# One tap of a depthwise convolution moved from VectorE to ScalarE and GpSimd, inside a state-space loop

## The chip, the cores and the metric

The kernel runs on one core of a Trainium2 chip. A core has a matrix engine (TensorE, PE in the profile, with PEld for its weight loads), VectorE (DVE), ScalarE (ACT), GpSimd (POOL) and SyncE (SP, which here issues DMAs). Each engine takes its instructions in order from its own queue; between engines they are ordered by semaphores. SBUF is the working memory on the chip, PSUM the accumulator memory of TensorE, in banks of 128 partitions x 512 floats.

The metric is the device time of one execution in microseconds. A separate profiled execution gives the trace.

## What is computed

Two layers of a sequence model over x, 64 sequences of 64 positions with 256 features, all float32. The first layer is a conditioned scan and an attention over the batch, then a modulated feed-forward net with quantised weights. The second layer is a tanh recurrence followed by a selective state-space block ("mamba"), and then two mixtures of experts. The change lies in the state-space block:

```python
xz = x @ W_in
xi, z = jnp.split(xz, 2, axis=-1)
xi_t = jnp.moveaxis(xi, 1, 2)
xi_pad = jnp.pad(xi_t, ((0, 0), (0, 0), (d_conv - 1, 0)))
conv = jax.lax.conv_general_dilated(xi_pad, W_conv, ..., feature_group_count=d_inner)
xc = jax.nn.silu(jnp.moveaxis(conv + b_conv[None, :, None], 2, 1))
dbc = xc @ W_xproj
delta_lr, B, C = jnp.split(dbc, [r, r + n], axis=-1)
delta = jax.nn.softplus(delta_lr @ W_dt + b_dt)
...
dA = jnp.exp(delta[..., None] * A)
dBx = delta[..., None] * B[:, :, None, :] * xc[..., None]
...
    h = dA_t * h + dBx_t
    y = jnp.einsum('bdn,bn->bd', h, C_t) + D * x_t
...
return y * jax.nn.silu(z) @ W_out
```

The inner width is 512, there are 16 states for each inner feature, and the convolution has four taps per feature (`d_conv` is 4), over the position: the value at position t is a weighted sum of positions t, t-1, t-2 and t-3, and positions before the first are zero.

## The kernel before

The 4096 tokens are cut into 8 chunks of 512 (8 whole sequences of 64). The 512 inner features are 4 blocks of 128 partitions (`NI = 4`), handled as two pairs (`PI = 2`). Function `mamba` runs over 8 chunks x 2 pairs x 16 states = 256 state steps.

A state step, for both blocks of the pair, consists of:
- an input: GpSimd multiplies `dx` by a state's B, spread over the partitions by a DMA (`inputs`, L1048, tile `hb`, five buffers, issued two steps ahead);
- a decay: ScalarE takes the exponential of delta times A into one of three PSUM banks (`decay`, L1055, tiles `dA0` to `dA2`, issued one step ahead; two banks are used by a step, so the second decay of the next step has to wait for a scan of this one);
- two scans on VectorE (L1100), one for each block, with the decay from PSUM and `hb` from SBUF;
- a multiply of both blocks by the state's C on VectorE (L1102); C is spread by a small matmul into the bank `cb` (L1000);
- a sum over the states on TensorE: eight transposing matmuls that accumulate in the banks `yp0` and `yp1` (L1115).

Beside the steps of a chunk, the loop places pieces of other work, a few at each step (`turn`, `pieces`, `urgent`, `others`): the head of the next chunk (`head`), the gates of this one (`gates`), its end (`finish`, `project`), and the shared expert of the mixture that follows (`mix.beside`, lines L1835 to L1855). A `yield` in these helpers marks where a piece ends.

The head of a chunk makes the convolution. For each of its four blocks, two matmuls fill the bank `mp` (L919; in the loop there is one such bank). ScalarE writes the last tap and the bias to `xc` (L923, `acc`). VectorE adds the three earlier taps, each shifted by one more position, straight from the bank (L926, 504, 496 and 488 elements per partition). After the fourth block, ScalarE takes the Silu of all four blocks (L930), which needs another table of ScalarE than the exponential of the decays, so that a table load stands before it and another before the next decay (L1055). Then TensorE projects `xc` (L934), and delta is made from the projection (L951 to L974), with the temporaries `t2` and `t3`, whose pool `p1` has a single buffer for each name. At the end of each pair of blocks, ScalarE also copies the sums out of their banks (L1127, `yT`).

The head of chunk 0 runs before the loop, with nothing beside it; the heads of chunks 1 to 7 run beside the steps of chunks 0 to 6. What follows an engine in its queue is settled when the program is built: a scheduler orders the instructions from the program and its own costs. The scans and the state multiplies are kept in the order of the program by a token (`stamp_issue_order_token`).

Of the kernel before, what the change touches and what calls it, by code (L numbers as in the profile page):

```python
# [13 lines left out]
F32 = mybir.dt.float32  # L14
BF16 = mybir.dt.bfloat16
I32 = mybir.dt.int32
AF = mybir.ActivationFunctionType
# [4 lines left out]
P = 128  # L22
B, L, D = 64, 64, 256
NT = B * L
CH = 512
# [835 lines left out]
def mamba(g, w, hs, beside):  # L861
# [3 lines left out]
    nc, tc = g.nc, g.tc  # L865
# [5 lines left out]
    PI = 2  # L871
# [5 lines left out]
    seq = lambda t: t.rearrange("p (b l) -> p b l", l=L)  # L877
    with (
# [30 lines left out]
        def head(c, v):  # L909

            tok = ts(c, CH)
            v.xc = p2.tile([P, NI, CH], F32, name="xc")
            v.delta, v.dx, v.sz, v.ready = [], [], [], 0
            v.dbc = p1.tile([W, CH], F32, name="dbc")
            v.parts = parts[c % 2]
            for i in range(NI):
                ps = one()
                for k in range(KD):
                    nc.tensor.matmul(ps, w.Win[:, k, ts(i, P)], hs2[:, k, tok], start=(k == 0), stop=(k == KD - 1))  # L919
                    if k == 0:  # L920
                        yield MID
                acc = v.xc[:, i, :]
                nc.scalar.activation(acc, ps, AF.Identity, bias=w.col[:, 0, i : i + 1], scale=w.taps[:, i, 3:4])  # L923
                for s in range(1, 4):
                    to = seq(acc)[:, :, s:]
                    nc.vector.scalar_tensor_tensor(  # L926
                        to, seq(ps)[:, :, : L - s], w.taps[:, i, 3 - s : 4 - s], to, ALU.mult, ALU.add
                    )
                yield
            nc.scalar.activation(v.xc, v.xc, AF.Silu)  # L930
            yield
            ps = one()
            for i in range(NI):
                nc.tensor.matmul(ps[:W, :], w.Wxp[:, i, :], v.xc[:, i, :], start=(i == 0), stop=(i == NI - 1))  # L934
                if i < NI - 1:
                    yield MID
            nc.scalar.copy(v.dbc, ps[:W, :])

            v.B = tc.dram_tile((S, CH), F32, name=f"B{c}")
            nc.sync.dma_start(v.B, v.dbc[R : R + S, :])  # L940


            r = slice(C0, W)
            nc.scalar.copy(v.parts[32 : 32 + S, :], ps[r, :])
            nc.vector.tensor_sub(ps[r, :], ps[r, :], v.parts[32 : 32 + S, :])
            nc.scalar.copy(v.parts[0:S, :], ps[r, :])
            nc.vector.tensor_sub(v.parts[64 : 64 + S, :], ps[r, :], v.parts[0:S, :])
            yield


            for i0 in range(0, NI, PI):  # L951
                z, u = (p3.tile([P, PI, CH], F32, name=n) for n in ("delta", "dx"))
                v.delta.append(z)
                v.dx.append(u)
                t2, t3 = (p1.tile([P, PI, CH], F32, name=n) for n in ("t2", "t3"))
                for i in range(PI):
                    ps = one()
                    nc.tensor.matmul(ps, w.Wdt[:, ts(i0 + i, P)], v.dbc[:R, :], start=True, stop=True)
                    nc.scalar.activation(z[:, i, :], ps, AF.Relu, bias=w.col[:, 1, i0 + i : i0 + i + 1])
                    nc.scalar.activation(u[:, i, :], ps, AF.Abs, bias=w.col[:, 1, i0 + i : i0 + i + 1])  # L960
                    yield
                e = nc.gpsimd if c else nc.vector
                nc.scalar.activation(u, u, AF.Exp, scale=-1.0)
                nc.scalar.activation(t2, u, AF.Identity, bias=unit[:, 0:1])
                nc.scalar.activation(t3, t2, AF.Identity, bias=unit[:, 1:2])
                yield
                e.tensor_sub(u, t3, u)
                yield
                nc.scalar.activation(t2, t2, AF.Ln)
                yield  # L970
                e.tensor_add(z, z, t2)
                yield
                e.tensor_sub(z, z, u)
                e.tensor_mul(u, z, v.xc[:, i0 : i0 + PI, :])  # L974
                v.ready += PI
                yield
# [85 lines left out]
        for _ in head(0, vs[0]):  # L1062
            pass
# [22 lines left out]
        for s in range(LAST):  # L1086
            c, j = divmod(s, STEPS)
            p, n = divmod(j, S)
            now = vs[c]
            if j == 0:  # L1090
                ahead = head(c + 1, vs[c + 1]) if c + 1 < NCH else iter(())
                pieces = chain(pieces, gates(c, now, 0), islice(ahead, 3 * NI + PI + 6), gates(c, now, PI), ahead)
                left = 0
# [1110 lines left out]
```

## Time and profile before

| | us |
|---|---|
| median of 3 runs | 2761.14 (2759.80 to 2762.74) |
| the profiled execution | 2768.27 |
| its span | 2766.5 |
| VectorE busy | 1766.7 (64%) |
| ScalarE busy | 1387.4 (50%) |
| GpSimd busy | 1338.1 (48%) |
| TensorE busy | 2320.8 (84%) |
| the state loop, first scan to the end of the last steps | 698.5 to about 1815 |

The granted clock of TensorE was 0.931 of full speed in the mean over the span. The shares above are averages over very different stages: before the state loop stand the scan, the attention and the feed-forward net, after it the two mixtures of experts. In the loop VectorE is the busiest; after it, TensorE.

A row of a group is "line engine operation, output<-inputs, shapes, xcount | busy us, mean ns of one | idle time of the engine just before them, and what ended it". A row of the waits is "engine line waited for <- what ended the wait: us in total, times, longest us". A row of the stretches gives for each engine its busy time and the number of its instructions, then the granted clock of TensorE, the share of the DMA engines and GB/s.

### The profile page before, as it was taken

The numbers are of one execution on the slowest core, as the hardware profiler recorded it, in microseconds if no ns is written. First come the engines' busy times: TensorE is split into PE (matmuls) and PEld (weight loads), VectorE is DVE, ScalarE is ACT, GpSimd is POOL, SyncE is SP. The second block draws the span as 40 slices with busy tenths as digits, with TensorE's granted clock in tenths as the row PEclk, the third lists the DMA queues.
The fourth block names the chain that finished last, engine by engine and source line by source line (L and its number), as shares of the span: only waits on it lengthen the run. The fifth ranks groups of instructions, "written<-read, shape, count | busy, mean of one in ns | idle before, by whom it ended". The sixth has DMA issues, their size and how long they took to land.

```text
span 2766.5 us, 34415 instructions
## 1 busy us (share of the span) xinstructions
PE 2320.8 (84%) x11977; PEld 1662.4 (60%) x11996; DVE 1766.7 (64%) x2980; ACT 1387.4 (50%) x2300; POOL 1338.1 (48%) x1166
## 2 busy tenths in 40 slices
PE   3989967997678888887888888788876989999995
PEld 3634435774345656564555555567655778888884
DVE  0567638982999898989889897952353443333333
ACT  0567527884575858585758576543222212222220
POOL 0023345530686878786888787835455331111110
PEclk9879988997769999999999999999998999999997
DMA  9999920002112222221122222226776755555555
GB/s 225 369 360 348 297 71 1 1 1 92 61 62 76 73 73 73 73 73 65 66 96 73 88 73 95 90 92 200 240 262 216 269 216 200 197 198 202 219 194 192
DMA packets 180503, 406.06 MB, mean 147 GB/s; under 512 B 24785, under 2 KB 84434, under 8 KB 174946
## 3 DMA queue, kind: packets, MB, share of 16 engines
q1 hardware_dynamic: 166882, 366.80, 38.9%
q0 software_dynamic: 13440, 36.98, 3.5%
q8 instruction: 97, 1.59, 0.2%
q14 instruction: 84, 0.69, 0.1%
HBM read 280.76 MB, written 144.98 MB: 154 GB/s over the span
## 4 chain that ended last, share of the span: by engine, by line
PE 45%; DVE 23%; ACT 12%; issue 9%; POOL 3%; another core or an unknown queue 2%; DMA 1%; SPq 0%; DVEq 0%; ACTq 0%; POOLq 0%
DVE hb L1100 13%; PE ps L1690 11%; PE acc L1588 9%; PE out L450 4%; DVE hb L1102 4%; PE ps L1657 2%; PE yp L1115 2%; ACT dA L1055 2%; PE mq L1835 2%; DVE xc L926 1%; PE s L416 1%; PE acc L441 1%; ACT L1055 1%; PE ps L1698 1%
## 5 line engine op out<-in xcount | busy, mean ns | idle before, releaser
L1048 POOL TENSOR_TENSOR hb<-dx,Bn 128x1024 f32<-128x1024 f32 x256 | 604.7, 2377 | 233.5 <-PE yp L1115 189.3
L1100 DVE TENSOR_TENSOR_SCAN hb<-dA,hb 128x512 f32<-128x512 f32 x512 | 602.1, 1208 | 62.0 <-ACT dA L1055 60.7
L1055 ACT ACTIVATE dA<-delta,negA 128x504 f32<-128x504 f32 x512 | 343.9, 682 | 284.9 <-DVE hb L1100 275.7
L1115 PEld LDWEIGHTS yp<-ident,hb 128*128 128x128 f32 x2048 | 261.1, 149 | 169.4 <-issue 134.9
L1102 DVE TENSOR_TENSOR hb<-hb,cb 128x1024 f32<-128x1024 f32 x256 | 311.9, 1219 | 44.1 <-PE cb L1000 25.1
L1690 PE MATMUL ps<-gxT,w 128*128 128x256 f32 (+1 forms) x1600 | 324.5, 361 | 1.4 <-DVE gxT L1565 0.8
L1690 PEld LDWEIGHTS ps<-gxT,w 128*128 128x128 f32 x1600 | 276.3, 190 | 47.6 <-issue 12.7
L1115 PE MATMUL yp<-ident,hb 128*128 128x128 f32 x2048 | 296.0, 288 | 0.0
L1835 PE MATMUL mq<-x,moe_s 128*128 128x256 f32 x896 | 242.3, 404 | 54.1 <-ACT up L1842 29.5
L1364 POOL DMA_INDIRECT ffn_y<-gy,to x72 | 69.3, 962 | 432.6 <-ACT gy L1590 420.1
L1835 PEld LDWEIGHTS mq<-x,moe_s 128*128 128x128 f32 x896 | 166.8, 199 | 120.8 <-ACT up L1842 35.8
L1694 DVE TENSOR_TENSOR gh<-gs,ps 128x256 f32<-128x256 f32 (+1 forms) x200 | 78.5, 394 | 212.5 <-ACT gs L1693 203.7
L1590 ACT ACTIVATE gy<-acc,wt 128x256 f32<-128x256 f32 x152 | 67.2, 473 | 250.4 <-PE acc L1588 224.2
L1588 PE MATMUL acc<-w,gh 128*128 128x256 f32 (+1 forms) x864 | 191.0, 392 | 0.0
L1693 ACT ACTIVATE gs<-ps 128x256 f32<-128x256 f32 (+1 forms) x200 | 72.2, 363 | 233.7 <-PE ps L1690 220.7
L1000 PE MATMUL cb<-parts,pick 80*128 80x512 bf16 x256 | 104.2, 407 | 87.0 <-DVE hb L1102 82.1
L1588 PEld LDWEIGHTS acc<-w,gh 128*128 128x128 f32 (+1 forms) x864 | 147.2, 192 | 31.0 <-issue 13.4
L432 POOL TENSOR_TENSOR E<-E,z 128x1024 f32<-128x1024 f32 x32 | 61.6, 1926 | 194.2 <-DVE z L431 111.4
L1364 POOL DMA_INDIRECT moe_y<-gy,to x80 | 77.6, 970 | 103.4 <-ACT gy L1590 79.4
L1588 PE MATMUL acc<-w,rh 128*128 128x256 f32 x320 | 86.0, 410 | 44.3 <-ACT rh L1659 41.5
L450 PE MATMUL out<-oT,hs 128*128 128x512 f32 x256 | 117.8, 604 | 1.5 <-ACT oT L443 1.5
L1578 DVE TENSOR_REDUCE wt<-pick 128x2 f32<-128x4 f32 (+1 forms) x88 | 13.6, 155 | 162.5 <-ACT gy L1590 144.0
(475 smaller groups left out, 4436.6 us busy)
## 6 DMA issues: line engine op xcount, KB each, us to landing
w<-ffn_w SPq DMA_DIRECT2D x40, 2176.0 KB
Bn<-B SPq DMA_DIRECT2D x128, 512.0 KB
moe_x<-fill SPq DMA_DIRECT2D x130, 260.0 KB
ffn_x<-fill SPq DMA_DIRECT2D x129, 260.0 KB
w<-moe_w SPq DMA_DIRECT2D x48, 512.0 KB
ffn_w<-in_ffn_W_dram SPq DMA_DIRECT2D x16, 640.0 KB
gx<-moe_x SPq DMA_DIRECT2D x32, 260.0 KB
gx<-ffn_x SPq DMA_DIRECT2D x32, 260.0 KB
```

What stands on the lines that cost most here:

```text
L450: nc.tensor.matmul(ps, M[:, o, ts(k, P)], v.o[:, o], start=(o == 0), stop=(o == H // 2 - 1))
L1000: nc.tensor.matmul(t, pick[:, n : n + 1].to_broadcast([rows, P]), v.parts, start=True, stop=True)
L1048: nc.gpsimd.tensor_mul(hb, vs[c].dx[p], Bn[:, n % NB, :].unsqueeze(1).to_broadcast([P, PI, CH]))
L1055: nc.scalar.activation(decays[s][i][:, :, 1:], seq(vs[c].delta[p][:, i, :])[:, :, 1:], AF.Exp, scale=A[:, p * PI + i, n : n + 1],)
L1100: ins = nc.vector.tensor_tensor_scan(h, dA[i].rearrange("p b l -> p (b l)"), h, 0.0, ALU.mult, ALU.add)
L1102: ins = nc.vector.tensor_tensor(hb, hb, cb.unsqueeze(1).to_broadcast([P, PI, CH]), ALU.mult)
L1115: nc.tensor.matmul(yp[i][:, t, :], hb[:, i, ts(t, P)], g.ident, start=(n == 0 and t == 0), stop=(n == S - 1 and t == CH // P - 1), is_tran ...
L1364: i = self.g.nc.gpsimd.indirect_dma_start(out=self.y, out_offset=bass.IndirectOffsetOnAxis(ap=to, axis=0), in_=y, in_offset=None)
L1588: nc.tensor.matmul(po[s], h, w, start=(i == 0), stop=(i == n - 1))
L1690: nc.tensor.matmul(ps[:, j, :], v.w12[:, k, ts(j * (full + 1) + i, P)], v.xT[:, k, :], start=(k == 0), stop=(k == KD - 1))
L1694: nc.vector.tensor_mul(v.h[:, i, : v.rows], s, ps[:, 1, :])
L1835: nc.tensor.matmul(ps[:, i % 2, :], w[:, k, ts(i, P)], xu[:, k, :], start=(k == 0), stop=(k == KD - 1))
```

## The change

In the heads of chunks 1 to 7 the first of the three taps (shift by one position, 504 elements) is no longer added by VectorE. ScalarE multiplies the bank by the tap's weights into a temporary `q`, which takes the buffers of `t2` (blocks 0 and 2) and `t3` (blocks 1 and 3). VectorE adds the other two taps as before. After the `yield`, so in a later piece, GpSimd adds the temporary to `xc`. The head of chunk 0 (`c` is 0) stays as it was.

```diff
                 acc = v.xc[:, i, :]
                 nc.scalar.activation(acc, ps, AF.Identity, bias=w.col[:, 0, i : i + 1], scale=w.taps[:, i, 3:4])
-                for s in range(1, 4):
+                many = 1 if c else 0
+                q = p1.tile([P, PI, CH], F32, name=("t2", "t3")[i % 2]) if c else None
+                for s in range(1, 1 + many):
+                    to = seq(q[:, s - 1, :])[:, :, s:]
+                    nc.scalar.activation(to, seq(ps)[:, :, : L - s], AF.Identity, scale=w.taps[:, i, 3 - s : 4 - s])
+                for s in range(1 + many, 4):
                     to = seq(acc)[:, :, s:]
                     nc.vector.scalar_tensor_tensor(
                         to, seq(ps)[:, :, : L - s], w.taps[:, i, 3 - s : 4 - s], to, ALU.mult, ALU.add
                     )
                 yield
+                for s in range(1, 1 + many):
+                    to = seq(acc)[:, :, s:]
+                    nc.gpsimd.tensor_add(to, to, seq(q[:, s - 1, :])[:, :, s:])
             nc.scalar.activation(v.xc, v.xc, AF.Silu)
```

Since the addition of the fourth block stands after its `yield`, it is written in the same piece as the Silu behind it, which reads what the addition wrote. The scheduler orders the whole program anew, so instructions near the head can stand in another order on every engine; line numbers behind the change grow by 8 (the scan is L1108, the Silu L938).

## The prediction

> **What bounds the kernel now.** I read the stretches of the state loop first, then the waits inside it, then the chain of waits through one head. The loop runs from 698.5 to 1815 us of a span of 2766.5.
>
> ```profile
> core 0: us, PE busy (x) PEld busy (x) DVE busy (x) ACT busy (x) POOL busy (x), PEclk, DMA share, GB/s
> 977.00:1116.00 139.00, 119.00 (x570) 79.57 (x569) 125.57 (x119) 99.53 (x134) 108.47 (x53) 0.99 0.21 73
> ...
> 1009.00:1047.00 38.00, 31.74 (x154) 21.43 (x153) 36.87 (x38) 26.88 (x35) 23.66 (x12) 1.00 0.16 56
> ```
>
> The first row is a whole chunk, the second the part of it in which the convolution of the next chunk's head runs. VectorE is busy 90% of the chunk and 97% of the convolution. TensorE follows with 84%, GpSimd has 62% there and ScalarE 71%.
>
> ```profile
> ACT dA L1055 <- DVE hb L1100: 275.7, 261, 5.4
> POOL hb L1048 <- PE yp L1115: 189.3, 97, 6.2
> DVE hb L1100 <- ACT dA L1055: 60.7, 41, 5.4
> DVE hb L1102 <- PE cb L1000: 25.1, 24, 3.2
> ```
>
> These are the waits inside the loop: total us, times, longest. ScalarE and GpSimd mostly wait for VectorE and for what follows it (275.7 and 189.3 us). VectorE itself waits 60.7 us for a decay, in 41 places. So VectorE sets the pace, except where ScalarE is held by something long.
>
> ```profile
> 1009.09 1.22 DVE hb L1102
> 1010.31 0.65 DVE xc L926
> 1010.96 1.13 DVE hb L1100
> 1012.09 0.63 DVE xc L926
> ...
> 1039.65 0.57 ACT dA L1055
> 1040.27 0.58 ACT yT L1127
> 1040.87 1.28 ACT L930
> 1042.16 1.91 ACT xc L930
> 1044.07 0.47 ACT yT L1127
> 1044.56 1.28 ACT L1055
> 1045.86 0.69 ACT dA L1055
> ...
> 1046.64 2.35 DVE hb L1100 x2
> ```
>
> This is the chain through that head (start, us, what). The taps (L926) stand on it, between scans and multiplies. Then it passes to ScalarE: table load, Silu of xc, table load back, decay. VectorE reaches the scan at 1046.64 only 0.44 us before that decay is there, so the last taps hide nearly all of the Silu block. That cover is what the change takes from.
>
> **The change, part by part.** Durations are of the profiled execution.
>
> ```profile
> L926 DVE SCALAR_TENSOR_TENSOR xc<-mp,taps,xc 128x504 f32<-128x504 f32 x28 | 20.3, 724 | 0.0
> L923 ACT ACTIVATE xc<-mp,mcol,taps 128x512 f32<-128x512 f32 x28 | 21.5, 769 | 11.5 <-PE mp L919 11.5
> L959 ACT ACTIVATE delta<-mp,mcol 128x512 f32<-128x512 f32 x28 | 19.0, 680 | 6.9 <-PE mp L958 6.9
> L1011 POOL TENSOR_TENSOR xc<-xc,sz 128x512 f32<-128x512 f32 x30 | 38.2, 1275 | 1.6 <-DVE xc L1010 1.6
> ```
>
> *Removed.* The 504-wide tap goes in the heads of chunks 1 to 7, four times each: 28 instructions (the head of chunk 0, ahead of the loop, keeps its three). Records overlap a little, so I count what the chain gives one tap before the next instruction, 0.62 to 0.75 us, mostly 0.65: 28 x 0.65 = 18.2 us. By the row's mean it would be 20.3 us, the most that can be had.
>
> *Added on ScalarE.* 28 scaled copies out of the bank. None is in the trace: below it stands the plain copy L1127 (0.58), above it L923 with a scale and a bias (0.77). I take 0.70, by L959 and by the decay L1055 (504 wide, scale, 0.68): 28 x 0.70 = 19.6 us. Over the convolution ScalarE waits 10.1 us for VectorE in front of decays, and that hides most of it; without this cover all 19.6 us would count. It is not hidden where ScalarE is just coming out of a table reload: in heads 2 to 4 after the shared expert's Silu (L1846, at 1014.59), where the built order puts a copy (and another bank read) ahead of the second decay; in heads 5 and 6 in the gate's Silu block, where the copy stands between the two loads. One copy each: 5 x 0.70 = 3.5 us lost. Bounds: 0 and 7 x 0.77 = 5.4.
>
> *Added on GpSimd.* 28 additions over 8 rows of 63. By L1011 and L1843, 512 wide, 1.27 us; bounded below by 0.95 (half of L432's 1.93 for 1024) and above by 2.37 (L1048, 1024 wide). I take 1.27, the nearest width: 35.6 us on a queue that idles 191.4 us in the loop before its multiplies. Scans wait for GpSimd 0.8 us in all, so the multiplies run well ahead and delay nobody. Behind an addition in the queue stand state multiplies (two steps ahead of need), the shared expert's L1843, and the convolution's own later additions. The third and fourth scaled copies wait until the first and second additions have let go of the temporary; in the built order some two state steps (over 7 us) lie between, against 3.6 us for a multiply and an addition: nothing.
>
> *The new wait.* The Silu of xc no longer waits for the last tap but for the last GpSimd addition, and ScalarE stands in order: behind Silu are two copies, the table reload and the next decay, for which the scan waits. No DMA moves, and no queue of SyncE is passed. I follow the built order from the scan (time 0) that frees the bank of the last decay before the block. VectorE then has a multiply, two scans, a multiply and a scan before it needs the first decay behind the block: 5 x 1.13 = 5.65 us, and each tap in between adds 0.64. ScalarE needs 0.05 + 0.69 + 1.28 + 1.91 + 2 x 0.58 + 1.28 + 0.69 = 7.06 us.
> In heads 2 to 4 both last taps now lie before time 0. GpSimd then has multiply, L1843, multiply and addition in a row (its buffers come free 2 us after each state multiply), so the addition ends at about 2.5 where Silu could start at 2.0: 0.5 us of wait. VectorE idles 7.06 + 0.5 - 5.65 = 1.9 us against 0.44 now: 1.4 lost, three times, 4.2.
> Head 1 has no copies of yT in the block and both last taps inside it (cover 6.9); the last tap ends at 2.4, the addition at 3.7, Silu at 5.6, the decay at 7.6: 0.7 lost against no idle now.
> Head 5: cover 6.3, chain 7.06 + 2 x 0.58 = 8.2, idle 1.9 against 2.31 at 1327.88: 0.4 won.
> Head 6: the shared expert's Silu and this one now stand in one block (one pair of table loads fewer): 7.06 + 1.91 + 0.58 = 9.55 against a cover of 6.9, idle 2.65, now 0.30: 2.3 lost.
> Head 7: the same block plus 1.0 us of wait for the addition, idle 3.65, now 3.53: 0.1 lost.
> Together 4.2 + 0.7 - 0.4 + 2.3 + 0.1 = 6.9 us.
>
> *Sum.* 18.2 - 3.5 - 6.9 = 7.8 us less. The profiled execution took 2768.27 us (span 2766.5), so it would take 2760.5; the median of the runs shown is 7.1 us below the profiled one, 2761.1, and becomes 2753.3.
>
> *A rule against it.* VectorE's scans took 1184 to 1225 ns and the state multiplies 1197 to 1223 throughout, while GpSimd was busy 108 of 139 us: no VectorE instruction was held up. The Trainium skill, Perfetto Trace Analysis, section Optimizing Scalar/DVE Operations, warns that moving work between GpSimd and VectorE might not help, because they share a read port of the SBUF. Its page SBUF — State Buffer, section SBUF: two separate sides, restricts the lock to VectorE instructions with two SBUF inputs or in a 2-port mode; the scan, the state multiply and the taps each read one operand from PSUM, and by that rule, too, the sum above stands. By the general warning it would come out as the last rival.
>
> **The rivals.** *The whole tap is won.* If the static order lets VectorE start its next work earlier and the Silu block finds other cover, all 18.2 us come: 2743. For it: 97% busy in the convolution. Against it: 0.44 us of slack in the block.
> *All given back.* If every head pays the worst of heads 2 to 6, that is 2.3 us in the Silu block, and a copy of 0.70 shows at one or two places, a head loses 2.3 to 3.7 of its 2.6: net about 0, 2761. TensorE, 84% busy over the convolution, can take part in this: where the taps gave it time, the state multiply would wait for its broadcast (L1000; 25.1 us now).
> *Slower: Silu stands behind GpSimd's queue.* The multiply ahead of the last addition waits for TensorE to empty its buffer. Such waits happen 97 times, 2.0 us in the mean and 6.2 at most, and I counted only a free buffer after 2 us. If the addition comes 2.4 us later in each head (one more L1048 ahead of it, or one such wait), ScalarE stands, the decay is late, and with 7 x 2.4 = 16.8 us the kernel is 9 us slower: 2770. It decides from 1.1 us a head on (7.8 / 7). For it: GpSimd is busy without a gap before the last addition in my count, and an addition of 2.37 us alone, two of them in that run, would bring 2.2. Against it: GpSimd sits idle 6.6 us in this part today.
> *The port is shared after all.* If each addition held a VectorE instruction for its 1.27 us, 35.6 us would be added: 2789. The even durations above speak against it.
> *Not doing what it says* has no chance of its own: the built program has 28 taps fewer on VectorE and 28 copies and additions more.
>
> **How the numbers follow.** Small gain (2750 to 2755.6) 0.47; whole tap 0.10; given back 0.24; slower by Silu's wait 0.16; port 0.03. A measurement of this kernel can tell about 0.2%, 5.5 us, from no change. So faster 0.57, same 0.24, slower 0.19. The range 2744 to 2770 leaves out the port, half of the slower case and a little of the whole tap; the cost bounds above (tap 20.3, copies 0 or 5.4, addition 0.95 or 2.37) stay inside it.
>
> **What would show it.** L926's successor with 68 instead of 96 instructions and VectorE about 18 us less busy in the loop; ScalarE's wait for VectorE falling by some 15 us; VectorE's wait for decays rising from 60.7 to about 70; scaled copies near 0.70 and additions near 1.27 us; Silu waiting under 1 us for GpSimd. Wrong would be additions above 2 us, waits of Silu above 1.1 us a head, or longer scans while GpSimd runs.

## The result

The changed kernel takes 2753.39 us in the median (2736.54 to 2763.35) against 2759.68 us before (2751.03 to 2763.21), 21 runs each. The medians differ by 6.3 us; 7.8 us less had been forecast. The ratio is 0.9973 with a 95% interval of 0.9960 to 0.9985, which is 4 to 11 us less. Here and below the ratio is an estimate of its own with an interval, and not quite the quotient of the two medians (0.9977 here). The forecast time of 2753.3 us is met to 0.1 us by chance: its base, 2761.1 us, was 1.4 us too high and its gain 1.5 us too large. The profiled execution of the changed kernel took 2753.39 us (span 2751.5), 15 us less than the one before. Only 6.8 us of this lie in the state loop, as the sums over its eight chunks show, cut from the loop's first scan to its last. The first is before, the second after:

```profile
sum 1114.60, PE 909.22 PEld 613.98 DVE 1005.70 ACT 749.70 POOL 867.03; mean PE 113.65 PEld 76.75 DVE 125.71 ACT 93.71 POOL 108.38
```

```profile
sum 1107.80, PE 902.00 PEld 612.62 DVE 988.91 ACT 759.82 POOL 900.54; mean PE 112.75 PEld 76.58 DVE 123.61 ACT 94.98 POOL 112.57
```

VectorE is busy 16.8 us less (1005.70 - 988.91). The loop is only 6.8 us shorter, so VectorE idles 10.0 us longer: this is the price. The other 8 us of the difference between the two profiles lie outside the loop, where the program is the same.

The groups of instructions in the loop after the change:

```profile
L937 POOL TENSOR_TENSOR xc<-xc,t 128x504 f32<-128x504 f32 x28 | 35.1, 1254 | 14.3 <-DVE xc L931 14.3
L931 DVE SCALAR_TENSOR_TENSOR xc<-mp,taps,xc 128x496 f32<-128x496 f32 x28 | 20.1, 719 | 0.0
...
L928 ACT ACTIVATE t<-mp,taps 128x504 f32<-128x504 f32 x28 | 18.8, 672 | 0.8 <-POOL xc L937 0.8
L938 ACT ACTIVATE xc<-xc 128x2048 f32<-128x2048 f32 x7 | 13.4, 1914 | 5.4 <-POOL xc L937 5.4
```

A scaled copy (L928) takes 0.672 us, an addition (L937) 1.254. The Silu (L938) now waits for the addition: 5.4 us in all, in five of seven heads. The waits of the loop:

```profile
ACT dA L1063 <- DVE hb L1108: 258.6, 241, 5.4
POOL hb L1056 <- PE yp L1123: 130.8, 65, 4.7
DVE hb L1108 <- ACT dA L1063: 67.7, 43, 5.4
DVE hb L1110 <- PE cb L1008: 24.7, 23, 3.2
```

ScalarE and GpSimd wait less than before (258.6 for 275.7, 130.8 for 189.3), since they have the added work. VectorE's wait for decays rises from 60.7 to 67.7 us. With its wait for ScalarE's `parts` in front of the split of the projection (L953; 2.8 us in place of 0.7) that is 9.1 of the 10.0 us. The place of it is seen in the chain through the head that the prediction followed (start, us, what):

```profile
1033.56 0.65 DVE xc L931
1034.21 1.13 DVE hb L1108
1035.34 0.62 DVE xc L931
1035.96 1.14 DVE hb L1108
...
1037.19 1.23 DVE hb L1110
1038.42 0.03 POOLq L1056
1038.45 0.83 POOL xc L937
1039.30 1.92 ACT xc L938
1041.22 0.95 ACT yT L1135 x2
1042.19 0.98 ACT L1063
...
1043.49 0.69 ACT dA L1063
1044.21 1.24 DVE hb L1108
```

Before, the chain went from the taps to ScalarE; now GpSimd's addition stands between them. VectorE idles 1.09 us ahead of the scan at 1044.21, against 0.44 before (the number in brackets is the idle time before an instruction):

```profile
1044.21 1.23 DVE L1108 TENSOR_TENSOR_SCAN hb<-dA,hb 128x512 f32<-128x512 f32 x1 [1.09 <-ACT dA L1063]
```

The chunk table below shows which other heads lose time.

### The profile page after: what moved, and what is told of

It is laid out like the page before. It is cut to its first block, busy times and chain, and to the rows that moved or that the text cites. A ratio compares the mean times of both kernels' runs of the same rounds, so it can differ in the third digit from the quotient of the medians.

```text
span 2751.5 us, 34452 instructions
## 1 busy us (share of the span) xinstructions
PE 2310.7 (84%) x11996; PEld 1659.9 (60%) x11996; DVE 1752.4 (64%) x2952; ACT 1398.3 (51%) x2324; POOL 1371.9 (50%) x1194
## 4 chain that ended last, share of the span: by engine, by line
PE 46%; DVE 22%; ACT 11%; issue 9%; POOL 4%; DMA 2%; another core or an unknown queue 1%; SPq 0%; DVEq 0%; ACTq 0%; POOLq 0%
DVE hb L1108 13%; PE ps L1698 11%; PE acc L1596 9%; PE out L450 4%; DVE hb L1110 3%; PE ps L1665 2%; PE mq L1843 2%; PE yp L1123 2%; ACT dA L1063 2%; PE steps L820 1%; PE s L416 1%; POOL hb L1056 1%; PE acc L441 1%; PE ps L1706 1%; PE mp L919 1%
## 5 line engine op out<-in xcount | busy, mean ns | idle before, releaser
L1056 POOL TENSOR_TENSOR hb<-dx,Bn 128x1024 f32<-128x1024 f32 x256 | 604.9, 2376 | 178.2 <-PE yp L1123 130.8
L1108 DVE TENSOR_TENSOR_SCAN hb<-dA,hb 128x512 f32<-128x512 f32 x512 | 602.3, 1210 | 68.5 <-ACT dA L1063 67.7
L1063 ACT ACTIVATE dA<-delta,negA 128x504 f32<-128x504 f32 x512 | 345.0, 685 | 265.4 <-DVE hb L1108 258.6
L1123 PEld LDWEIGHTS yp<-ident,hb 128*128 128x128 f32 x2048 | 260.1, 149 | 158.4 <-issue 125.2
L1110 DVE TENSOR_TENSOR hb<-hb,cb 128x1024 f32<-128x1024 f32 x256 | 312.4, 1220 | 45.1 <-PE cb L1008 24.7
L1123 PE MATMUL yp<-ident,hb 128*128 128x128 f32 x2048 | 294.6, 286 | 0.0
L1843 PE MATMUL mq<-x,moe_s 128*128 128x256 f32 x896 | 238.2, 399 | 57.8 <-ACT sh L1847 25.8
L1843 PEld LDWEIGHTS mq<-x,moe_s 128*128 128x128 f32 x896 | 164.3, 196 | 124.1 <-ACT sh L1847 42.9
L1008 PE MATMUL cb<-parts,pick 80*128 80x512 bf16 x256 | 103.3, 404 | 89.2 <-DVE hb L1110 83.3
L1859 PE MATMUL mq<-moe_s,sh 128*128 128x256 f32 x448 | 113.3, 386 | 6.6 <-ACT up L1850 2.9
```

Source lines behind the costliest of these rows:

```text
L1008: nc.tensor.matmul(t, pick[:, n : n + 1].to_broadcast([rows, P]), v.parts, start=True, stop=True)
L1056: nc.gpsimd.tensor_mul(hb, vs[c].dx[p], Bn[:, n % NB, :].unsqueeze(1).to_broadcast([P, PI, CH]))
L1063: nc.scalar.activation(decays[s][i][:, :, 1:], seq(vs[c].delta[p][:, i, :])[:, :, 1:], AF.Exp, scale=A[:, p * PI + i, n : n + 1],)
L1108: ins = nc.vector.tensor_tensor_scan(h, dA[i].rearrange("p b l -> p (b l)"), h, 0.0, ALU.mult, ALU.add)
L1110: ins = nc.vector.tensor_tensor(hb, hb, cb.unsqueeze(1).to_broadcast([P, PI, CH]), ALU.mult)
L1123: nc.tensor.matmul(yp[i][:, t, :], hb[:, i, ts(t, P)], g.ident, start=(n == 0 and t == 0), stop=(n == S - 1 and t == CH // P - 1), is_tran ...
```

## The experiments

What follows an engine in its queue is settled anew for each program, so a kernel with one piece less may also stand in another order. The length of each chunk (from its first scan to the next chunk's first scan; chunk k holds the head of chunk k+1, the last chunk holds none) tells where a difference arises. Two kernels with the same order up to some point agree there to about 0.1 us, as long as TensorE is not late (below). The experiments ran in three groups on three chips, on which the kernel before took 2722.05, 2759.63 and 2720.59 us. So a time is compared only with that of the kernel before in its own group; the loop of the kernel before was 1114.6 us long on the third chip too. The table is in us, from one traced execution of each kernel; all rows but the first are differences from the first:

| chunk | 0 | 1 | 2 | 3 | 4 | 5 | 6 | 7 | loop |
|---|---|---|---|---|---|---|---|---|---|
| before | 132.5 | 138.6 | 138.3 | 139.0 | 149.6 | 140.4 | 146.1 | 130.1 | 1114.6 |
| the change | -1.6 | 0.3 | -0.8 | -2.3 | -2.2 | 0.4 | 0.1 | -0.7 | -6.8 |
| heads 1 to 5 only | -2.0 | -2.4 | -1.7 | -2.4 | -3.3 | 0.0 | 0.6 | 0.1 | -11.1 |
| heads 6 and 7 only | -0.1 | 0.0 | 0.1 | -0.1 | -0.1 | 0.6 | 0.0 | -0.7 | -0.4 |
| tap gone | -2.3 | 1.5 | 2.2 | 0.9 | -1.2 | -1.0 | -3.8 | -0.7 | -4.6 |
| price alone | 2.0 | -1.0 | -0.2 | -0.5 | -1.8 | 2.2 | 4.4 | 10.0 | 15.0 |
| no wait | -1.7 | 1.9 | 1.0 | 1.3 | -3.0 | 0.6 | -2.5 | -0.6 | -2.9 |
| added twice | -2.1 | 5.1 | 5.1 | 4.4 | 2.4 | 5.5 | 5.1 | 9.7 | 35.3 |
| last block kept | -1.2 | -1.6 | -2.4 | -1.7 | -2.5 | -0.2 | -2.0 | 9.7 | -1.9 |
| no copy | -1.2 | -1.6 | -2.3 | -0.3 | -0.4 | -1.0 | 2.1 | 9.5 | 4.8 |
| last kept, table by ScalarE | -1.1 | -1.6 | -2.4 | -1.7 | -2.4 | -0.2 | -3.2 | -0.8 | -13.6 |
| the change, table by ScalarE | -1.5 | -1.0 | -1.7 | -2.4 | -2.4 | -0.4 | -0.1 | -0.8 | -10.3 |
| before, table by ScalarE | 0.0 | 0.0 | 0.1 | -0.1 | 0.0 | 0.0 | 0.7 | -0.8 | 0.0 |
| mixed, table by ScalarE | -1.9 | -2.4 | -1.7 | -2.4 | -3.3 | -0.1 | -3.1 | -0.8 | -15.7 |

### Which heads win

```diff
-                many = 1 if c else 0
+                many = 1 if 0 < c < 6 else 0
```

> The tap is moved in the heads of chunks 1 to 5 only; heads 6 and 7 keep three taps on VectorE. My theory: each head wins about 2.4 us of VectorE work (16.8 us over seven heads in the profile) and pays by its own ScalarE block; heads 6 and 7 pay about 3.0 and 2.5 us and so win nothing. Then these five heads carry the whole gain: ratio to before about 0.9975 (0.996 to 0.999), and the chunks with heads 6 and 7 are as long as before within 0.5 us. Rival (the gain is the same for every tap moved): 20 of 28 taps, 4.5 us, ratio 0.9984.

Measured: 2705.47 us against 2722.05, ratio 0.9953 (0.9936 to 0.9970). That is more gain than the range expected (0.996 to 0.999). The other part, with `many = 1 if c > 5 else 0`:

> The other part alone: the tap is moved in the heads of chunks 6 and 7 only. My theory: 4.8 us of VectorE work are won and some 5.5 us are given back because the Silu of xc now follows the shared expert's Silu in one block on ScalarE, so that the decay is later: ratio 1.0000 to 1.0005, and VectorE's idle time in those two chunks rises by 4 to 6 us. Rival (each tap gives the same): 8 of 28 taps, 1.8 us less, ratio 0.9993.

Measured: 2720.78 us, ratio 1.0000 (0.9991 to 1.0010). In the loop heads 1 to 5 bring all of the gain (11.8 us in chunks 0 to 4) and heads 6 and 7 nothing, as the theory said; in chunks 5 and 6 of the second kernel VectorE idles 5.6 us longer than before.

It was not expected that heads 1 to 5 alone win more than the whole change does there (11.8 against 6.6 us in chunks 0 to 4), though in these chunks the order of instructions is the same on every engine. The stretches show it, chunks 1 to 3 of the change first, then those of the kernel with heads 1 to 5:

```profile
831.00:969.90 138.90, 119.16 (x558) 81.11 (x558) 122.58 (x114) 100.32 (x136) 109.65 (x56) 0.95 0.21 71
969.90:1107.40 137.50, 119.35 (x568) 80.24 (x568) 122.75 (x114) 100.83 (x137) 112.29 (x57) 0.98 0.21 73
1107.40:1244.10 136.70, 116.76 (x568) 78.52 (x568) 122.74 (x115) 100.83 (x137) 113.21 (x57) 1.00 0.22 74
```

```profile
825.80:962.10 136.30, 116.73 (x558) 79.11 (x558) 122.60 (x115) 100.16 (x136) 108.94 (x56) 0.98 0.23 74
962.10:1098.60 136.50, 116.74 (x568) 78.51 (x568) 122.58 (x114) 100.64 (x137) 113.01 (x57) 1.00 0.23 74
1098.60:1235.20 136.60, 116.74 (x568) 78.51 (x568) 122.69 (x114) 100.66 (x137) 113.09 (x57) 1.00 0.23 74
```

VectorE's busy time is the same (122.6 to 122.7). What differs is the granted clock of TensorE, the number behind POOL's instructions: 0.95 and 0.98 in the change's chunks 1 and 2, where its matmuls take 2.4 and 2.6 us more and the chunk is 2.6 and 1.0 us longer. The timeline near the end of chunk 1, the change first, then heads 1 to 5 at the same place:

```profile
958.08 1.91 PE L1843 MATMUL mq<-x,moe_s 128*128 128x256 f32 x4
...
960.08 0.59 ACT L1850 COPY xr<-mq 128x512 f32<-128x512 f32 x1 [2.79 <-PE mq L1843]
960.57 1.30 ACT L1063 ACTIVATE dA<-delta,negA 128x504 f32<-128x504 f32 x2
...
961.36 2.34 DVE L1108 TENSOR_TENSOR_SCAN hb<-dA,hb 128x512 f32<-128x512 f32 x2 [1.49 <-ACT dA L1063]
```

```profile
952.24 0.59 ACT L1850 COPY xr<-mq 128x512 f32<-128x512 f32 x1
952.72 1.29 ACT L1063 ACTIVATE dA<-delta,negA 128x504 f32<-128x504 f32 x2
...
954.61 2.33 DVE L1108 TENSOR_TENSOR_SCAN hb<-dA,hb 128x512 f32<-128x512 f32 x2
```

The shared expert's matmul (L1843) is late, ScalarE stands before its copy for 2.79 us, the decays behind the copy are late, and VectorE waits 1.49 us here and 1.31 us at 966.34, together 2.80. With the matmul in time nobody waits. A chunk's mean clock hides how this comes about. In every trace of this case the granted clock is either 1 or 0.5, and in chunks 1 to 3 the stretches at 0.5 last 3.4 us or a multiple of it. In the change two of them in a row lie on this matmul; with heads 1 to 5 moved there is none here.

The wait is not new. The kernel before has such a stretch of 3.4 us in the last quarter of each of chunks 1 to 3, in all three traces with its order there (before, heads 6 and 7 only, before with the table by ScalarE). The stretch in the change, the one in chunk 1 before, and what follows from the latter:

```profile
953.70:960.50 6.80, 5.92 (x17) 4.27 (x17) 5.03 (x5) 4.01 (x6) 3.41 (x2) 0.50 0.00 0
```

```profile
955.80:959.20 3.40, 3.40 (x14) 2.73 (x12) 2.46 (x3) 2.36 (x4) 1.59 (x2) 0.50 0.00 0
```

```profile
959.80 0.59 ACT L1842 COPY xr<-mq 128x512 f32<-128x512 f32 x1 [1.64 <-PE mq L1835]
...
961.07 2.34 DVE L1100 TENSOR_TENSOR_SCAN hb<-dA,hb 128x512 f32<-128x512 f32 x2 [0.33 <-ACT dA L1055]
...
966.04 2.34 DVE L1100 TENSOR_TENSOR_SCAN hb<-dA,hb 128x512 f32<-128x512 f32 x2 [1.31 <-ACT dA L1055]
```

So before, VectorE loses about 1.6 us to it in chunks 1 and 3, and 0.9 us in chunk 2, where ScalarE waits 0.75 us for the matmul and VectorE's longest wait for a decay is 5.37 us instead of the 4.51 of chunks 1 and 3. In the execution with heads 1 to 5 moved all of this is gone. The change's own trace is rid of it in chunks 2 and 3, loses 2.80 us in chunk 1 and 0.78 us to another late matmul (L1033) in chunk 2. Since the order is the same, the difference between the two lies in the execution and not in the kernel. In the execution with the change's order and another place of one small copy (below), VectorE lost 1.5 us to this in chunk 1 and nothing in chunks 2 and 3. What decides whether the clock falls there, these runs do not show.

### The removal alone, and the price alone

"Tap gone" leaves out the copy, the addition and the tap. "Price alone" has all three taps on VectorE and the copy and addition too.

```diff
-                q = p1.tile([P, PI, CH], F32, name=("t2", "t3")[i % 2]) if c else None
-                for s in range(1, 1 + many):
-                    nc.scalar.activation(...)
...
-                    nc.gpsimd.tensor_add(...)
```

> The tap is left out altogether in heads 1 to 7: no scaled copy, no addition, the result lacks this tap. This is the removal without its price. My theory: VectorE is busy 17 us less, and only the lost cover of the Silu block is given back (about 3 to 6 us): 11 to 14 us less than before, ratio 0.9955 (0.995 to 0.9965). Rival (the freed time goes to TensorE or to its clock, whatever is added): not more than the 6.3 us of the change, ratio 0.9977. Rival (the price lies in GpSimd's wait alone): all 17 us, ratio 0.9938.

```diff
-                for s in range(1 + many, 4):
+                for s in range(1, 4):
```

> The scaled copies and GpSimd's additions as in the change, while VectorE keeps its three taps too, so this tap counts twice in the result. This is the price without the gain. My theory: VectorE's busy time as before, the price some 3 to 7 us (copies behind table loads, Silu's wait for the last addition, with the third tap still covering part of it): ratio 1.0018 (1.0005 to 1.003). Rival (GpSimd's additions hold up VectorE's instructions through a shared port): 35 us, ratio 1.013, with scans and taps that last longer. Rival (the added work is hidden wholly): 1.0000.

Measured: tap gone 2717.92 us, ratio 0.9989 (0.9979 to 0.9999); price alone 2732.28 us, ratio 1.0040 (1.0024 to 1.0056). Both expectations were missed. Without the tap and without its price the loop wins 4.6 us, less than the change itself, as the rival with TensorE and its clock had it. One reason is the order: Silu, which waits for nothing now, stands a piece earlier, and with it the projection behind it. Head 3 of this kernel:

```profile
1033.61 3.32 PE L935 MATMUL mp<-xc,Wxp 128*48 128x512 f32 x4
...
1039.87 0.58 ACT L938 COPY dbc<-mp 48x512 f32<-48x512 f32 x1 [2.16 <-PE mp L935]
1040.47 0.58 ACT L945 CAST parts<-mp 16x512 bf16<-16x512 f32 x1
...
1041.08 0.69 DVE L946 TENSOR_TENSOR mp<-mp,parts 16x512 f32<-16x512 f32 x1 [2.14 <-ACT parts L945]
```

VectorE's next instruction in its queue is one of the head's own (L946, the split of the projection), which needs ScalarE's `parts`; it idles 2.14 us before it, where nothing was waited for in head 3 before. The other reason is the clock: it is 0.53 from 1033.00 to 1036.60, and the first four matmuls of the projection (L935) take 3.32 us there, where all eight took 3.63 before. No run separates the two. So a removal without the added work is not an upper bound of the gain here. The price alone comes to 5.3 us without the 9.7 of the last chunk, which have a cause of their own (below). The sum agrees with the 3 to 7 expected, by one profile, but the place was not expected: heads 1, 6 and 7 pay 8.6 us, while chunks 1 to 4 are 3.5 us shorter than before.

### The wait of Silu for GpSimd

Three kernels: additions that nobody waits for (`to` is the scaled copy itself), each addition made twice, and the tap of the last block left on VectorE.

```diff
-                    to = seq(acc)[:, :, s:]
-                    nc.gpsimd.tensor_add(to, to, seq(q[:, s - 1, :])[:, :, s:])
+                    to = seq(q[:, s - 1, :])[:, :, s:]
+                    nc.gpsimd.tensor_add(to, to, to)
```

> As the change, with the same copies and as many additions of the same size on GpSimd, but each addition doubles the scaled copy instead of adding it to xc: Silu waits for nobody on GpSimd, and the tap is missing in the result. My theory: the 5.4 us for which Silu waits for GpSimd go, and 2 to 5 us of it reach the end: 8 to 11 us less than before, ratio 0.9965 (0.996 to 0.997). Rival (Silu's wait is not on the path): like the change, ratio 0.9977.

```diff
-                for s in range(1, 1 + many):
+                for s in (1, 1) if many else ():
                     to = seq(acc)[:, :, s:]
                     nc.gpsimd.tensor_add(to, to, seq(q[:, s - 1, :])[:, :, s:])
```

> As the change, but GpSimd adds the scaled copy twice, so the tap counts twice in the result; 28 more additions of 1.25 us, and Silu waits for one more of them. My theory: in each of the seven heads ScalarE's block starts up to 1.25 us later and VectorE idles as much longer, 5 to 9 us given back: ratio 0.999 to 1.001, scans no longer than 1.21 us. Rival (GpSimd's lateness is hidden): 0.9977. Rival (additions hold up VectorE): 35 us more, 1.010.

```diff
-                many = 1 if c else 0
+                many = 1 if c and i < NI - 1 else 0
```

> As the change in the first three of the four blocks of a head; the fourth keeps all three taps on VectorE, so Silu waits for VectorE's last tap as before and GpSimd's additions lie well ahead. 21 taps move. My theory: 12.6 us of VectorE work are won, the wait of Silu for GpSimd is gone and one tap more covers the block, so 5 us at most are given back: 7.5 to 10 us less than before, ratio 0.9968. Rival (the gain goes with the number of taps): three quarters of 6.3 us, ratio 0.9983.

Measured: no wait 2767.85 us against 2759.63, ratio 1.0026 (1.0008 to 1.0044); added twice 2795.47 us, 1.0125 (1.0108 to 1.0142); last block kept 2755.42 us, 0.9976 (0.9960 to 0.9991). The first two miss what was expected; the interval of the third holds both its 0.9968 and the rival's 0.9983.

The change wins 6.3 us; with each addition made twice, 34.5 us are lost (0.0125 x 2759.63). ScalarE's wait before Silu and head 3 of this kernel:

```profile
ACT xc L938 <- POOL xc L937: 24.0, 6, 6.6
```

```profile
1043.93 2.57 POOL L937 TENSOR_TENSOR xc<-xc,t 128x504 f32<-128x504 f32 x2
...
1046.53 1.91 ACT L938 ACTIVATE xc<-xc 128x2048 f32<-128x2048 f32 x1 [4.04 <-POOL xc L937]
...
1051.43 1.22 DVE L1108 TENSOR_TENSOR_SCAN hb<-dA,hb 128x512 f32<-128x512 f32 x1 [4.93 <-ACT dA L1063]
```

One more addition of 1.25 us a head at the end makes Silu wait 24.0 instead of 5.4 us, since GpSimd, with 28 additions more in its queue, also comes to it later, and VectorE idles 4.93 us before the scan instead of 1.09. That is not the whole loss. Another 9.7 us are the last chunk's (below), and of the 31.6 us by which chunks 0 to 6 are longer than in the change only 18.6 are Silu's longer wait. In head 3 VectorE also waits 1.5 us for the next broadcast (L1008) and 1.7 us behind the shared expert's late matmul, and the order differs from the change in this kernel too. The scans stay as they were (median 1.214 us, 1.216 in the change), so they are not held up by GpSimd. Silu's wait is on the path, then: 1.25 us more work a head made it 2.7 us longer a head.

With the last block kept on VectorE, ScalarE does not wait for GpSimd at all, and VectorE has no gap at head 3's Silu block. Chunks 0 to 6 are 11.6 us shorter than before with three quarters of the taps moved, the change with all of them 6.1 us. In heads 6 and 7 this is the last block's doing: 2.2 us won against 0.5 lost. In heads 1 to 5 it is 9.4 us against 6.6, where the change's trace has TensorE's lateness; the change's order in another execution won 9.0 there, and 11.8 in the one with no such lateness in chunks 1 to 3. "No wait" falls on the other side: in its traced execution the loop wins 2.9 us, with the new wait for `parts` in six places (9.7 us in all), as in "tap gone". That execution took 2752.28 us, 15.6 below the kernel's median, and what makes the others longer is not in the trace; it stays open. The long copy of the last chunk (below) could be a part of it, which no run tests.

### The scaled copies

```diff
-                    nc.scalar.activation(to, seq(ps)[:, :, : L - s], AF.Identity, scale=w.taps[:, i, 3 - s : 4 - s])
...
-                    nc.gpsimd.tensor_add(to, to, seq(q[:, s - 1, :])[:, :, s:])
+                    nc.gpsimd.tensor_add(to, to, to)
```

> As the change, but without the scaled copies on ScalarE: GpSimd adds xc to itself at the same size and place, so the result lacks the tap and doubles the rest. My theory of the prediction: the copies cost 3.5 us where ScalarE comes out of a table load, so this is 9 to 11 us less than before, ratio 0.9965. Rival (the copies are hidden): like the change, 0.9977. Rival (copies cost their full 19 us): 0.991.

Measured: 2763.62 us, ratio 1.0011 (0.9996 to 1.0025), so the expectation was missed. Without the copies nothing is won: chunks 0 to 6 are 4.7 us shorter than before, those of the change 6.1. The order differs here too (chunks 3 and 4 win 0.3 and 0.4 us, and chunk 6 loses 2.1; in chunk 3 ScalarE waits 2.80 us for the shared expert's matmul, in chunk 6 Silu waits 4.02 us for GpSimd), so this sets no exact price, but 3.5 us of cost that would come back are not seen. In the change's traces with no late matmul, VectorE has no gap in heads 2 to 4 behind the shared expert's Silu, where a copy was expected to show.

### The last chunk: one copy of 9.9 us

In four of the eight kernels so far the last chunk, which holds no convolution, is 9.5 to 10 us longer. Nearly all of it (9.3 to 9.7 us) is one instruction, VectorE's conversion of a table of 128x48 numbers to integers (L1411). It takes 0.18 us in the change; with the last block kept the timeline shows:

```profile
1734.70 0.96 POOL L1357 DMA_INDIRECT moe_x<-rows,moe_row  x1 [0.30 <-issue]
1735.08 9.89 DVE L1411 CAST moe_tiles<-tilesf 128x48 int32<-128x48 f32 x1
1735.68 9.23 POOL L1056 TENSOR_TENSOR hb<-dx,Bn 128x1024 f32<-128x1024 f32 x4
...
1744.88 2.32 DVE L1108 TENSOR_TENSOR_SCAN hb<-dA,hb 128x512 f32<-128x512 f32 x2
```

The copy starts while GpSimd issues an indirect DMA, and ends when GpSimd has done four state multiplies without a gap. In the change it happened to fall between two of those DMAs. It was given to ScalarE, with all else in the same order (the line makes four such copies in the program, which all went):

```diff
-        nc.vector.tensor_copy(table, lists)
+        nc.scalar.copy(table, lists)
```

> The kernel with the last block's tap kept on VectorE, and the integer copy of a table of tiles (L1411, 128x48) made by ScalarE in place of VectorE; every other instruction stands in the same order as there. Theory: this copy took 9.89 us instead of 0.18 because VectorE had to wait until GpSimd had finished four state multiplies (9.23 us); on ScalarE it cannot, so the last chunk is 129.5 to 130.5 us long instead of 139.9, and the ratio goes from 0.9976 to about 0.9942 (0.993 to 0.9955). Rival (the long copy only shows a wait that something else sets anyway): ratio as there, 0.9976, last chunk near 140 us.

> The changed kernel with the same integer copy made by ScalarE, order otherwise as in the change. The profiled execution of the change showed the copy at 0.18 us, so by the profile nothing changes: 0.9973 (0.996 to 0.9985). If the copy falls into GpSimd's multiplies in a part of the executions (the times of the change are spread over 27 us, those before over 12 us), the ratio comes to 0.9940 to 0.996 and the spread of the times halves. ScalarE's decays wait no longer than before (the copy is about 0.2 us).

> The kernel before with the same integer copy made by ScalarE and nothing else, as the footing for the other two. In the profile before the copy took 0.17 us: ratio 1.0000 (0.9990 to 1.0010). Rival (ScalarE's place for it matters, or the copy waits in some executions before as well): off from 1 by over 0.1%.

> All four taps moved in heads 1 to 5, the first three in heads 6 and 7 (their last block keeps its tap on VectorE), and the integer copy on ScalarE. By the chunks of the runs so far: 11.8 us less in heads 1 to 5 (as where only these were moved), 2.2 us less in heads 6 and 7 (as with the last tap kept): 14 us less, ratio 0.9949 (0.993 to 0.9965). Rival (the order settled anew moves the loss elsewhere): as the change, 0.9973, with VectorE idle in other places.

Against 2720.59 us before: last block kept 2709.67 us, ratio 0.9965 (0.9952 to 0.9978); the change 2709.93 us, 0.9968 (0.9955 to 0.9982); the kernel before 2719.66 us, 1.0005 (0.9992 to 1.0017); mixed (`many = 1 if c and (c < 6 or i < NI - 1) else 0`) 2708.07 us, 0.9959 (0.9945 to 0.9974). The last chunk with the last block kept, VectorE's copy first, ScalarE's second:

```profile
1672.10:1812.00 139.90, 106.92 (x555) 79.00 (x555) 128.55 (x145) 73.03 (x106) 102.89 (x64) 0.95 0.25 83
```

```profile
1672.60:1801.90 129.30, 104.73 (x553) 77.64 (x553) 119.32 (x144) 73.09 (x106) 102.02 (x63) 0.99 0.27 90
```

10.6 us less in this chunk, in the trace; the ratio moves only from 0.9976 to 0.9965, less than the 0.9942 expected, with intervals that overlap, and on another chip. So the copy's wait is shown, and its worth over all executions is not: it need not be there in each. Whether it hits the change in some of its 21 runs stays open; its ratio is 0.9973 with the copy on VectorE and 0.9968 on ScalarE, which the intervals don't tell apart.

The mixed kernel's loop is 15.7 us shorter than before (14 were worked out). It and the one with heads 1 to 5 alone have the lowest ratios, but the change's interval overlaps with theirs, so that they beat it too is not shown by the times. By the chunks the mixed kernel wins 2.7 us over the change's order on the same chip in heads 6 and 7, where the kernels differ, and as much in chunks 0 to 4, where only the execution does.

## Why the prediction held, point by point

*What bounds the loop.* VectorE, with ScalarE's long blocks: right. TensorE was named only in a rival, and there as a later loss. It costs 4.1 us in chunks 1 to 3 of the kernel before and 3.6 us in chunks 1 and 2 of the traced execution of the change, so the sum lacked a term that can go either way.

*Removed: 18.2 us.* VectorE is busy 16.8 us less, 0.60 a tap instead of 0.65.

*Copies: 0.70 us each, 3.5 lost.* They take 0.672. The loss was not found in heads 2 to 4, where three of the five were counted; heads 5 and 6 together cost as forecast, without showing which part of it is a copy. The term was too high by about 2.

*Additions: 1.27 us each, no delay of others.* They take 1.254. The third and fourth copies wait 0.8 us in all for the first and second.

*Silu's wait: under 1.1 us a head.* It is 5.4 us in seven heads, 0.77 in the mean, but two heads are above the limit that the prediction set. In head 7 it was 3.1 instead of the 1.0 counted, because the addition there stands behind two state multiplies. In head 1 it was 1.7, where the sum's times (last tap at 2.4, addition at 3.7) allow 1.3; in heads 2 to 4 0.19 each in place of 0.5.

*Silu's cover: 6.9 us.* The idle time of VectorE in front of the first scan behind the Silu block, in us:

| head | 1 | 2 to 4, each | 5 | 6 | 7 |
|---|---|---|---|---|---|
| before | 0 | 0.44 | 2.31 | 0.30 | 3.53 |
| forecast | 0.7 | 1.9 | 1.9 | 2.65 | 3.65 |
| measured | 0.67 | 1.09 | 1.36 | 2.22 | 5.42 |

That is 5.5 us lost at this place, not 6.9. By heads, the idle time of VectorE in their chunks (length less busy time, after less before) against what the prediction makes lost there, its copies included:

| head | 1 | 2 | 3 | 4 | 5 | 6 | 7 | none | sum |
|---|---|---|---|---|---|---|---|---|---|
| forecast | 0.7 | 2.1 | 2.1 | 2.1 | 0.3 | 3.0 | 0.1 | 0 | 10.4 |
| measured | 0.9 | 2.5 | 1.3 | 0.0 | 0.4 | 3.0 | 2.5 | -0.6 | 10.0 |

The sum is right partly by luck. Head 1 is as worked out from the built order. Heads 5 and 6 come out in the sum only: their blocks idle about 0.5 us less than counted, and the rest is lost elsewhere in the chunk (in head 6, 0.83 us before the split of the projection). In heads 2 to 4 the block loses 0.65 us each instead of the 1.4 counted, and what is lost is won back later in the chunk, where ScalarE no longer waits for the shared expert's matmul as it did before. Where TensorE is in time (head 4 here, heads 2 to 4 with heads 1 to 5 moved) the chunk idles 0.5 us longer at most. What was seen in heads 2 and 3 is mostly TensorE's lateness. Head 7 lost 2.4 us more than counted: 1.8 in the block, by GpSimd's queue, and 0.5 in front of L1519, which by the profile waits for a DMA. So the mis-sized terms are the cover of heads 2 to 4 and their copies (6.3 us counted, 0.3 in the kernel with heads 1 to 5) and head 7.

*The rivals.* The whole tap is not won. "All given back" was right that TensorE takes part, but not about where: the state multiply's wait for its broadcast is 24.7 us (25.1 before), and the late matmul is the shared expert's. "Slower: behind GpSimd's queue" is real, in heads 1 and 7 of the change and in six heads with each addition made twice. There Silu waits 24.0 us and the kernel is 1.25% slower, 9.7 us of it by the copy in the last chunk. In the mean the change stays below the limit (0.77 of 1.1 us a head). The port: beside GpSimd's additions scans and state multiplies last as long as before (medians of 1.216 and 1.222 us; 1.212 and 1.221 before), and so do the 496-wide taps (0.719 us in the mean, 0.723 before). What GpSimd did hold up is one copy with both operands in SBUF; that the port is the cause of it is not shown by a run.

## What to carry to other kernels

An addition given to an idle engine costs by the place it takes in the chain, not by its length. Where that engine's queue is late just before a long dependent block, as in heads 6 and 7 here, leave the last piece where it was and move the others; in heads 1 to 5 moving all four did about as well or better (9.0 and 11.8 us against 9.2 and 9.4). Where a scheduler orders the program anew, compare stage by stage between kernels; leaving work out is then no upper bound. And when the busiest engine gets faster by 2%, look at once at which engine was second, in the trace before as well: here stretches of 3.4 us at half clock on TensorE added or removed up to 2.8 us a chunk, in executions with the same order of instructions.

## What the runs showed of the hardware

A VectorE copy of 128x48 floats to integers, with both operands in SBUF, took 9.89 us instead of 0.18, until four GpSimd multiplies of 2.3 us, back to back, were over. On ScalarE the same copy took 0.21 us. The Trainium skill, SBUF — State Buffer, section SBUF: two separate sides, says that a VectorE operation in a mode with two ports and a GpSimd operation exclude each other for a whole instruction. The trace agrees in that VectorE is blocked, and here the wait lasted through four instructions in a row.

The granted clock of TensorE took two values in the 14 traces, 1 and 0.5. In chunk 1 eight transposing matmuls of a state step (L1123) took 1.91 us in the change, at 0.5, and 1.04 us with heads 1 to 5 moved, at 1.
